# Four chained image layers on one core: the sparse last taps of two 3x3 convolutions as 64x64 products, beside two halves of a 1x1 mixing

## The chip, the core and the metric

The kernel runs on one core of a Trainium2 chip. A core has five engines, each with its own queue of instructions: TensorE (PE, matrix products; its weight loads are listed apart as PEld), VectorE (DVE), ScalarE (ACT), GpSimd (POOL) and SyncE (SP, which issues most DMA transfers). The engines wait for one another through semaphores. Operands lie in SBUF, 128 partitions wide; products accumulate in PSUM, also 128 partitions wide, of which the kernel uses eight banks of 512 fp32 columns (its pools add up to them).

The metric is the device time of one execution in microseconds (us). A trace records when each instruction and each DMA packet started and how long it took.

## The reference

Sixteen images of 64 channels and 128x128 pixels pass four layers. Each adds a function of its group-normalized input (32 groups of two channels) to its input:

```python
x = x + einsum('oc,bchw->bohw', conv_w, gram(gn(x)) applied to gn(x))   # layer 0: 1x1 mixing
x = x + abs(sobel_x(gn(x))) + abs(sobel_y(gn(x)))                       # layer 1: 3x3, per channel
x = x + conv3x3(shift(gn(x)), W) + b                                    # layer 2: quarter of channels
                                                                        # shifted left, quarter right
x = x + clip(leaky(batchnorm(conv1x1(conv3x3(gn(x), w_bin), w1x1))), 0, 255)   # layer 3
```

All is fp32. The batch normalization of layer 3 runs over all images, so its last part can only begin when every image has passed the products.

## The kernel before, in words

**Staging.** An image is cut into eight pieces (`NS`), and one step of the main loop (lines 1051 to 1099) works on one piece of each stage: `Front` (layers 0 and 1) of one image, `Layer2` of an image that is ten steps older, `Layer3` of one that is twenty steps older, and `Gram` (the Gram matrix of an image to come). A step has four quarters, `q` = 0 to 3. In each quarter the stages run in the order Layer3, Layer2, Front; then "last of" parts of Layer2 (quarters 0 and 3), then Gram, then `tick()`, which moves the chains of small statistics on by a link. Every engine executes in the order of the program (`InOrder`). When all images are through, a last loop normalizes, clips, adds and stores, bound to DMA.

**The products of layers 2 and 3.** Rows are worked in pairs, and a 3x3 kernel over pairs is written with sums and differences of planes: `difference` (DVE, line 698) puts into `d2` or `d3` the difference of two neighbouring planes, slot 0 and slot 1, and products of differences and of whole planes add up to the output `two` (two PSUM banks, slot 0 and slot 1). `one` is a third bank, for the shared plane (`shared`, three products on each half of the output channels). `own` (line 745) issues the products of one slot. Of the two output halves (64 partitions each) one has a whole 128x64 weight and takes three products, the taps kx = 1, 0, 2. The other half has only one plane with weights, so of its 128 weight rows 64 are zero. There, two taps are packed into one product (`pk`, which reads a copy of the difference, `qd`, the "twin", shifted by one pixel in one half), and the third, the **last tap**, remains a 128x64 product of which half the rows are zero. In all five products per slot.

**How products run.** A product of 64 output columns takes a half of the array; `issue` (line 722) holds products of both halves in queues and emits them in turns, so that two run side by side. `issue_rest` empties the queues before Front's products in quarters 1 and 3. An fp32 product appears in the trace as two passes.

**When.** Layer 3: `shared` and `own` of slot 0 in quarter 0, `own` of slot 1 in quarter 1; `y`, the sum read from `two` by DVE, in quarter 2, then the differences of the next piece in quarters 2 and 3. Layer 2: `shared` and `own` of slot 1 in quarter 2, `own` of slot 0 in quarter 3; the difference of slot 1 for the next piece ("last of 3", line 911) at the end of quarter 3; then, in quarter 0, the first two Sobel operations of the front, an addition at the row edges, `x`, the sum read from `two` (line 840), and the difference of slot 0. The twin of a layer 2 difference is made by two POOL-issued DMAs (line 802), that of layer 3 by two ACT copies. `d2`, `d3` and their twins have one buffer each.

**The mixing.** `abd` is a block-diagonal 128x128 weight (two copies of the 64x64 mixing, for the upper and lower half of the image). For the first three images (`EARLY`) `mix` issues whole 128x64 products, two in quarter 1 and two in quarter 3. For images 3 to 15 (`four`), `load` places a chunk so that rows 0 to 63 of the array get one four-row group of both image halves and rows 64 to 127 the other, and `mix_four` (line 571) issues four 64x64 products in quarter 1, one on each quadrant of the array: group 0 writes the bank `po`, group 1 the bank `g`. ACT normalizes them into `xh` (`prepare`): group 0 in quarter 2 of the same step, group 1 in quarter 0 of the next one.

Of the kernel before, what the change touches and what calls it, by code (L numbers as in the profile page):

```python
# [16 lines left out]
P = 128  # L17
# [3 lines left out]
R = 8  # L21
NS = HH // R
EARLY = 3
CP = 4
# [85 lines left out]
def tile_kernel(ctx: ExitStack, tc: tile.TileContext, x, cw_h, w2_t, b2, wbin_t, w1_t, b1, gamma, beta, consts, out):  # L110
# [56 lines left out]
    def cols(o):  # L167
        return slice(o * C, (o + 1) * C)
# [372 lines left out]
    class Front:  # L541
# [14 lines left out]
        def load(self, i):  # L556
            b = self.b
            t = xin.tile([P, R, W], F32, tag="x", name=f"x_{b}_{i}")
            if self.four:

                t = t.rearrange("p (h r) w -> p h r w", h=2)
                v = x[b].rearrange("c (h r) w -> c h (r w)", h=2)
                for g in range(2):
                    j = (i * R + g * CP) * W
                    sp.dma_start(t[cols(g)].rearrange("p h r w -> p h (r w)"), v[:, :, j:j + CP * W])
            else:
                for h in range(2):
                    sp.dma_start(flat(t[h * C:(h + 1) * C]), halves(x[b].rearrange("c h w -> (c h w)"), h, i * R, R))
            self.xs[i] = t

        def mix_four(self, i):

            for g, (pool, tag) in enumerate(((ps_po, "po"), (ps_g, "g"))):
                self.po[i, g] = pool.tile([P, CP, W], F32, tag=tag, name=f"po_{self.b}_{i}_{g}")
            t = self.xs.pop(i)
            order = 1 - last[0], last[0]
            for g in range(2):
                for h in order:
                    pe.matmul(self.po[i, g][cols(h)], self.abd[cols(g), cols(g)], t[cols(g), h], start=True, stop=True)

        def mix(self, i, g):
            if self.b == 0 and (i, g) in ((0, 1), (1, 0)):
# [15 lines left out]
        def at(self, i, q):  # L598
            b = self.b
            if q == 0:  # L600
                if i == -3:

                    self.xe = xin.tile([P, W], F32, tag="xe", name=f"xe_{b}", bufs=1)
                    sp.dma_start(self.xe[lo], x[b][:, HH, :])
                    sp.dma_start(self.xe[hi], x[b][:, HH - 1, :])
                    sp.dma_start(x2_d[b][0:W].rearrange("(p w) -> p w", p=1), w0[0:1, 0:W])
                if i + 3 < NS and i + 3 not in self.xs:
                    self.load(i + 3)
                if -1 <= i < NS - 1:
                    self.prepare(i + 1, 1)  # L610
                if 1 <= i:
                    self.store(i - 1)
                    act.activation(
                        junk.rearrange("p (j w) -> p j w", w=W), self.x2.pop(i - 1), AF.Square,
                        accum_out=self.st[:, 1, i - 1:i],
                    )
                if i == NS:
                    chains.append(coefficients(self.st, lambda co: coefs2.update({b: co}), b2_sb))
            if q == 1 and -2 <= i < NS - 2:
                if i == -2:  # L620
                    self.abd, self.co = lead.pop(b)
                if i == -2 and not self.four:
                    self.pe = ps_g.tile([P, CP, W], F32, tag="g", name=f"pe_{b}")[:, 0, :]
                    small_product(self.pe, self.abd, self.xe)
                if self.four:
                    self.mix_four(i + 2)
                else:
                    self.mix(i + 2, 0)
            if q == 3 and i == -2 and self.four:
                self.pe = ps_po.tile([P, CP, W], F32, tag="po", name=f"pe_{b}")[:, 0, :]  # L630
                small_product(self.pe, self.abd, self.xe)
            if (i, q) == ((-1, 0) if self.four else (-2, 2)):
                nc.gpsimd.memset(self.chunk(0)[lo, 0, :], 0.0)
                self.normalized(self.chunk(0)[hi, 0, 1:1 + W], self.pe[hi], hi)
                self.pel = small.tile([P, W], F32, tag="pel", name=f"pel_{b}", bufs=1)
                self.normalized(self.pel[lo], self.pe[lo], lo)
            if q == 2:
                if i == NS - 2:
                    nc.gpsimd.memset(self.chunk(NS - 1)[hi, R + 1, :], 0.0)
                    act.copy(self.chunk(NS - 1)[lo, R + 1, 1:1 + W], self.pel[lo])  # L640
            if 0 <= i < NS:
                self.sobel(i, q)
            if q == 2 and -2 <= i < NS - 2:
                self.prepare(i + 2, 0)
            if q == 3 and -2 <= i < NS - 2 and not self.four:
                self.mix(i + 2, 1)
                self.xs.pop(i + 2)

        def sobel(self, i, q):
# [69 lines left out]
        pe.matmul(dst, wt, src, start=start, stop=stop)  # L719
        last[0] = o  # L720

    def issue(halves):


        for o in range(2):
            for n, (dst, wt, src) in enumerate(halves[o]):
                held[o].append((dst, wt, src, n == 0, n + 1 == len(halves[o])))
        while held[0] and held[1]:
            o = 1 - last[0]
            emit(o)  # L730
            emit(1 - o)
# [10 lines left out]
    def shared(p, wt, t, m=CP):  # L742
        products(p[:, 0:m], [wt], [by_parity(t)[1][:, 0:m]])

    def own(p, n, table, wt, name, m=CP, both=None):
        d, q, pk = diffs[name][:, n, 0:m], twins[name][:, n, 0:m], packed[f"pk{name[1]}"][:, n]
        o, _ = single(table, n)
        some = [None, None]
        some[1 - o] = taps(1 - o, p[:, 0:m], [wt[:, n] if both is None else both], [d], 1)
        some[o] = [  # L750
            (p[cols(o), 0:m], pk, q[:, :, 1:1 + W]),
            (p[cols(o), 0:m, 0:W - 1], wt[:, n, 2, cols(o)], d[:, :, 2:1 + W]),
        ]
        issue(some)


    tiles3 = {}

    class Layer2:
# [65 lines left out]
        def at(self, i, q):  # L825
# [51 lines left out]
            if q == 2:  # L877
                if 0 <= i < NS:
                    t = self.v[i]
                    one = ps_one.tile([P, CP, W], F32, tag="one", name=f"one2_{b}_{i}")  # L880
                    two = ps_two.tile([P, 2, CP, W], F32, tag="two", name=f"two2_{b}_{i}")
                    self.p[i] = two, one
                    shared(one, self.wi[:, 0], t, m)
                    if closing:
                        small_product(one[:, m, :], w0, t[:, R, :])

                    both = self.wi[:, 1]
                    own(two[:, 1], 1, TO_SLOTS, w2, "d2", m, both)
                    if closing:

                        p = two[:, 1, m:CP]
                        issue([taps(0, p, [both], [t[:, R:R + 1, :]]), taps(1, p, [both], [t[:, R - 1:R, :]])])

                    self.c = ring.tile([P, CP * W], F32, tag="c2", name=f"c2_{b}_{i}", bufs=1)
                    act.activation(self.c, flat(one), AF.Identity, bias=self.co[:, 5:6])
                if 1 <= i < NS:
                    self.square(i - 1)
                if 1 <= i:
                    self.store(i - 1)
            if q == 3:  # L900
                if 0 <= i < NS:
                    t = self.v.pop(i)
                    two, one = self.p[i]
                    both = self.wi[:, 1]
                    own(two[:, 0], 0, TO_SLOTS, w2, "d2", m, both)
                    if closing:
                        p, srcs = two[:, 0, m:CP], [t[:, R - 2:R - 1, :], t[:, R - 1:R, :]]
                        issue([taps(0, p, [w2[:, 0], both], srcs), taps(1, p, [both, w2[:, 1]], srcs)])
            if q == "last of 0" and i == NS:
                self.square(i - 1)  # L910
            if q == "last of 3" and -1 <= i < NS - 1:
# [4 lines left out]
    class Layer3:  # L916
# [34 lines left out]
        def at(self, i, q):  # L951
# [10 lines left out]
            if q == 1:  # L962
                if 0 <= i < NS:
                    two, one = self.p[i]
                    own(two[:, 1], 1, TO_PAIRS, w3, "d3")
                    self.v.pop(i)
                    self.c = ring.tile([P, CP * W], F32, tag="c3", name=f"c3_{b}_{i}", bufs=1)
                    act.activation(self.c, flat(one), AF.Identity, bias=b1_sb)
                if i + 1 < NS:
                    self.prepare(i + 1)  # L970
                if 1 <= i:
                    y = self.y.pop(i - 1)
                    for s in range(2):
                        for z in range(2):
                            v = pairs(y_d[b], s)[:, (i - 1) * R:i * R, :].rearrange("c (n z) w -> c z n w", z=2)
                            sp.dma_start(v[:, z], y[s * C:(s + 1) * C, z])
# [74 lines left out]
    for step in range(starts[2][1] - 2, steps):  # L1051
        now[0] = step
        for q in range(4):
# [5 lines left out]
            for stage, at in starts:  # L1059
                if stage is Front and q in (1, 3):  # L1060
                    issue_rest()
                for b in range(B):
                    run(stage, b, step - at - NS * b, q)
            if q in (0, 3):
                for b in range(B):
                    run(Layer2, b, step - starts[1][1] - NS * b, f"last of {q}")
# [116 lines left out]
```

## Time and profile before

| | |
|---|---|
| runs of the kernel | 2716.34, 2716.12, 2712.99 us; median 2716.12 |
| the profiled execution | 2713.5 us |
| its span, first to last instruction | 2711.7 us |
| PE busy | 2146.4 us (79% of the span), 14804 passes |
| DVE busy | 2116.7 us (78%) |
| ACT busy | 2069.4 us (76%) |
| POOL busy | 1042.6 us (38%) |
| mean granted PE clock | 0.899 |
| HBM traffic | read 346.23 MB, written 268.44 MB |
| passes of the mixing in 64x64 products | 832, 615 ns each |

A line of a timeline gives the start in us from the span's first instruction, the duration, the engine, the line, the operation, the tile written and the tiles read, their shapes, and how many instructions are merged (x8); in square brackets stands the engine's idle time before it and what released it ("issue": nothing that the profile shows). Nearly all instructions have the line L73, that of the wrapper that keeps the order, so they are told apart by tiles: `d<-v` is a difference, `qd<-d` its twin, `two<-d,w`, `two<-d,wi` and `two<-qd,pk` are products of the slots (in layer 2 with `wi`, which has the normalization of the image folded in), `one<-v,w` and `one<-v,wi` begin layer 3 and layer 2 on PE, `po<-x,abd` is the mixing, `bank<-xw` a Gram product, `u` and `e` are the Sobel's tiles. Passes are pipelined: a pass of 512 columns lasts 0.59 us, and the next one of the same half starts 0.43 us after it.

The chain that ended last is no help here: followed back from the end it lies in the DMA-bound last part. The stage before it, from 330 to 2000 us, has to be read step by step.

### The profile page before, as it was taken

How to read it: one execution, taken by the hardware profiler on the slowest of the kernel's cores; microseconds unless marked ns; L12 is line 12 of the kernel's file. 1: busy time of each engine (PE TensorE's matmuls, PEld its weight loads, DVE VectorE, ACT ScalarE, POOL GpSimd, SP SyncE). 2: the span in 40 equal slices, each digit the busy share in tenths (PEclk: the TensorE clock that was granted, in tenths of full speed). 3: DMA queues.
4: the chain of work that ended last, by engine and by line, in shares of the span. 5: the costliest groups of instructions: out<-in, count | busy, mean ns of one | idle time of the engine just before them, and what ended most of it. 6: DMA issues, size and time to landing. Idle time of an engine off the chain costs nothing. (4 is left out here: it accounts for less than half of the span.)

```text
span 2711.7 us, 45518 instructions
## 1 busy us (share of the span) xinstructions
PE 2146.4 (79%) x14804; PEld 905.4 (33%) x14804; DVE 2116.7 (78%) x3111; ACT 2069.4 (76%) x3001; POOL 1042.6 (38%) x1558
## 2 busy tenths in 40 slices
PE   6578899999999999999999999999999992000000
PEld 4234433434343434343434343333335641000000
DVE  4998899898989898989898999999994335333332
ACT  4766889898989898989899989999996666333332
POOL 2266545444445454444445454655554300000000
PEclk8689999999999999999999999999999996555555
DMA  8799889998999889898989888888887879999999
GB/s 208 204 236 241 223 197 245 225 237 222 236 225 241 227 230 230 227 231 232 229 228 237 214 216 204 212 216 218 220 204 187 219 197 327 420 420 420 420 420 374
DMA packets 693596, 685.92 MB, mean 253 GB/s; under 512 B 60096, under 2 KB 580448, under 8 KB 693360
## 3 DMA queue, kind: packets, MB, share of 16 engines
q1 hardware_dynamic: 668208, 613.83, 79.0%
q0 software_dynamic: 25152, 69.18, 10.0%
q8 instruction: 119, 1.95, 0.3%
q14 instruction: 117, 0.96, 0.1%
HBM read 346.23 MB, written 268.44 MB: 227 GB/s over the span
## 5 line engine op out<-in xcount | busy, mean ns | idle before, releaser
L73 PE MATMUL two<-d,w 128*64 128x508 f32 (+2 forms) x2560 | 835.7, 586 | 0.0
L73 PE MATMUL two<-d,wi 128*64 128x508 f32 (+3 forms) x1536 | 571.7, 576 | 0.0
L73 PE MATMUL two<-qd,pk 128*64 128x512 f32 (+1 forms) x1024 | 517.4, 586 | 25.7 <-DMA qd<-d 25.3
L73 POOL DMA_DIRECT2D qd<-d x512 | 272.3, 534 | 686.5 <-DVE d L73 277.9
L73 POOL TENSOR_SCALAR edges<-v,co 64x8 f32<-64x8 f32 x512 | 328.7, 642 | 274.7 <-ACT v L73 195.1
L73 DVE TENSOR_TENSOR d<-v 128x512 f32<-128x512 f32 (+1 forms) x512 | 346.7, 680 | 86.0 <-issue 50.4
L73 PEld LDWEIGHTS two<-d,w 128*64 128x64 f32 x2560 | 272.4, 136 | 322.8 <-issue 282.7
L73 PE MATMUL one<-v,w 128*64 128x508 f32 (+2 forms) x1600 | 364.4, 579 | 1.1 <-ACT v L73 1.1
L73 PE MATMUL one<-v,wi 128*64 128x508 f32 (+3 forms) x1536 | 355.8, 595 | 0.4 <-DVE wi L73 0.3
L73 ACT COPY qd<-d 64x512 f32<-64x512 f32 x512 | 315.6, 616 | 23.3 <-DVE d L73 13.8
L73 DVE SCALAR_TENSOR_TENSOR e<-e 128x1032 f32<-128x1032 f32 (+1 forms) x256 | 313.3, 1224 | 0.0
L73 ACT ACTIVATE xh<-po,co 128x128 f32<-128x128 f32 (+1 forms) x480 | 275.5, 624 | 28.9 <-PE po L73 25.0
L73 PEld LDWEIGHTS two<-d,wi 128*64 128x64 f32 x1536 | 178.6, 135 | 201.3 <-issue 183.2
L73 POOL TENSOR_SCALAR v<-v,kc 128x9 f32<-128x9 f32 x256 | 229.9, 912 | 12.0
L73 DVE SCALAR_TENSOR_TENSOR y<-two,c 128x1024 f32<-128x1024 f32 x128 | 156.0, 1219 | 98.0 <-ACT v L73 45.5
L73 PE MATMUL po<-x,abd 64*64 64x512 f32 (+1 forms) x1024 | 176.6, 639 | 43.9 <-ACT xh L73 38.2
L73 ACT ACTIVATE v<-x,co 128x1024 f32<-128x1024 f32 (+3 forms) x256 | 203.9, 847 | 0.0
L73 ACT ACTIVATE u<-u 128x1024 f32<-128x1024 f32 x128 | 135.6, 1060 | 81.6 <-DVE u L73 80.1
L73 ACT ACTIVATE c<-one,co 128x512 f32<-128x512 f32 x128 | 87.0, 679 | 140.2 <-PE one L73 140.1
L73 PEld LDWEIGHTS two<-qd,pk 128*64 128x64 f32 x1024 | 135.2, 136 | 164.6 <-issue 104.8
L73 PEld LDWEIGHTS one<-v,w 128*64 128x64 f32 x1600 | 130.5, 136 | 175.9 <-issue 147.3
L73 DVE SCALAR_TENSOR_TENSOR u<-xh 128x1170 f32<-128x1170 f32 x128 | 175.5, 1371 | 5.6 <-ACT xh L73 4.5
(160 smaller groups left out, 3432.1 us busy)
## 6 DMA issues: line engine op xcount, KB each, us to landing
x<-in_x SPq DMA_DIRECT2D x256, 256.0 KB, 4.7
x_d<-u SPq DMA_DIRECT2D x512, 128.0 KB, 4.1
y_d<-y SPq DMA_DIRECT2D x512, 128.0 KB, 3.5
x_d<-x SPq DMA_DIRECT2D x496, 128.0 KB, 3.1
xr<-in_x SPq DMA_DIRECT2D x120, 512.0 KB, 6.0
qd<-d POOLq DMA_DIRECT2D x256, 130.0 KB, 3.2
qd<-d POOLq DMA_DIRECT2D x256, 129.8 KB, 3.8
v<-x_d SPq DMA_DIRECT2D x448, 72.1 KB, 2.8
```

The lines of the kernel that those rows point to most:

```text
L73: return self.tc.keep_in_program_order(call(*args, **kwargs))
```

## The change

The last taps leave `own`. `last_taps` collects them in a list, `sparse`, as soon as a layer's last slot is issued. `mix_four` no longer issues anything: for one four-row group it collects the two 64x64 products on the diagonal of the array (image half h to output half h, both into one bank) in the list `beside`, group 0 in quarter 1, group 1 in quarter 3. `issue_sparse`, after the stages of a quarter, issues both lists: the two last taps as 64x64 products with their 64 weight rows alone, which lie off the diagonal, then the two mixing products. So layer 3's last taps run with group 0 at the end of the second quarter, layer 2's with group 1 at the end of the fourth. Where nothing is mixed that way (the first three images, and after the front is through) the last taps are issued as a pair of 128x64 products, as before but at that later place. `load` places a chunk of every image as it did for the first three, in two transfers with runs of 4 KB instead of 2 KB. `issue`, `own` and the closing rows of layer 2 pass on whether an accumulation is still open.

```diff
-            if self.four:
-                t = t.rearrange("p (h r) w -> p h r w", h=2)
-                v = x[b].rearrange("c (h r) w -> c h (r w)", h=2)
-                for g in range(2):
-                    j = (i * R + g * CP) * W
-                    sp.dma_start(t[cols(g)].rearrange("p h r w -> p h (r w)"), v[:, :, j:j + CP * W])
-            else:
-                for h in range(2):
-                    sp.dma_start(flat(t[h * C:(h + 1) * C]), halves(x[b].rearrange("c h w -> (c h w)"), h, i * R, R))
+            for h in range(2):
+                sp.dma_start(flat(t[h * C:(h + 1) * C]), halves(x[b].rearrange("c h w -> (c h w)"), h, i * R, R))
...
-        def mix_four(self, i):
-            for g, (pool, tag) in enumerate(((ps_po, "po"), (ps_g, "g"))):
-                self.po[i, g] = pool.tile([P, CP, W], F32, tag=tag, name=f"po_{self.b}_{i}_{g}")
-            t = self.xs.pop(i)
-            order = 1 - last[0], last[0]
-            for g in range(2):
-                for h in order:
-                    pe.matmul(self.po[i, g][cols(h)], self.abd[cols(g), cols(g)], t[cols(g), h], start=True, stop=True)
+        def mix_four(self, i, g):
+            pool, tag = ((ps_po, "po"), (ps_g, "g"))[g]
+            po = pool.tile([P, CP, W], F32, tag=tag, name=f"po_{self.b}_{i}_{g}")
+            t = self.xs[i][:, g * CP:(g + 1) * CP, :]
+            for h in range(2):
+                beside.append((po[cols(h)], self.abd[cols(h), cols(h)], t[cols(h)], True, True))
+            self.po[i, g] = po
...
-                    self.mix_four(i + 2)
+                    self.mix_four(i + 2, 0)
...
-            if q == 3 and -2 <= i < NS - 2 and not self.four:
-                self.mix(i + 2, 1)
+            if q == 3 and -2 <= i < NS - 2:
+                if self.four:
+                    self.mix_four(i + 2, 1)
+                else:
+                    self.mix(i + 2, 1)
                 self.xs.pop(i + 2)
...
+    sparse, beside = [], []
+    def issue_sparse():
+        if beside:
+            for (dst, wt, src, o, i), other in zip(sparse, beside):
+                pe.matmul(dst, wt[cols(i)], src[cols(i)], start=False, stop=True)
+            for dst, wt, src, start, stop in beside:
+                pe.matmul(dst, wt, src, start=start, stop=stop)
+            last[0] = 1
+        else:
+            for dst, wt, src, o, i in sorted(sparse, key=lambda made: made[3] == last[0]):
+                pe.matmul(dst, wt, src, start=False, stop=True)
+                last[0] = o
+        sparse.clear()
+        beside.clear()
...
-        some[o] = [
-            (p[cols(o), 0:m], pk, q[:, :, 1:1 + W]),
-            (p[cols(o), 0:m, 0:W - 1], wt[:, n, 2, cols(o)], d[:, :, 2:1 + W]),
-        ]
-        issue(some)
+        some[o] = [(p[cols(o), 0:m], pk, q[:, :, 1:1 + W])]
+        issue(some, (False, False), [more or h == o for h in range(2)])
+    def last_taps(two, table, wt, name, m=CP):
+        for n in range(2):
+            o, i = single(table, n)
+            sparse.append((two[cols(o), n, 0:m, 0:W - 1], wt[:, n, 2, cols(o)], diffs[name][:, n, 0:m, 2:1 + W], o, i))
...
+                    last_taps(two, TO_SLOTS, w2, "d2", m)
...
                     own(two[:, 1], 1, TO_PAIRS, w3, "d3")
+                    last_taps(two, TO_PAIRS, w3, "d3")
...
                 for b in range(B):
                     run(stage, b, step - at - NS * b, q)
+            issue_sparse()
             if q in (0, 3):
```

## Prediction

> **What bounds the kernel now.** I read the page first. Over most of the span TensorE (PE), VectorE (DVE), ScalarE (ACT) and the DMA engines are all eight or nine tenths busy, so a share of busy time names no limit. Then I cut the trace into steps. A step is one round of the main loop: eight row pairs of the 3x3 layer ("layer 3" here, the fourth of the reference), eight of the shifted one ("layer 2"), one chunk of the front. It begins here where DVE starts layer 2's late difference, `difference("d2", 1)`. This is the windows view of the eight steps that handle one image (columns: length, busy us with instructions of PE, PE's weight loads, DVE, ACT, POOL, then PE clock, DMA share, GB/s):
>
> ```profile
> 969.10:983.70 14.60, 14.60 (x72) 4.88 (x70) 14.38 (x20) 14.50 (x23) 7.26 (x11) 1.00 0.88 244
> 983.70:998.60 14.90, 14.90 (x82) 4.91 (x80) 14.80 (x23) 14.81 (x23) 5.69 (x11) 1.00 0.83 201
> 998.60:1014.10 15.50, 15.50 (x152) 6.83 (x150) 15.24 (x27) 13.41 (x21) 7.51 (x12) 1.00 0.89 225
> 1014.10:1032.20 18.10, 18.10 (x170) 8.10 (x168) 16.32 (x27) 14.44 (x24) 5.66 (x10) 1.00 0.76 186
> 1032.20:1050.30 18.10, 18.10 (x178) 7.96 (x176) 15.74 (x28) 13.67 (x22) 8.18 (x13) 1.00 0.94 239
> 1050.30:1065.70 15.40, 15.40 (x99) 6.41 (x97) 14.63 (x23) 15.30 (x23) 10.80 (x16) 1.00 0.95 245
> 1065.70:1085.10 19.40, 19.40 (x118) 9.23 (x115) 15.89 (x26) 18.33 (x31) 8.59 (x12) 1.00 0.97 246
> 1085.10:1099.90 14.80, 13.10 (x66) 4.02 (x62) 14.73 (x24) 14.55 (x22) 8.16 (x11) 1.00 0.94 242
> sum 130.80, PE 129.10 PEld 52.34 DVE 121.72 ACT 119.02 POOL 61.84; mean PE 16.14 PEld 6.54 DVE 15.22 ACT 14.88 POOL 7.73
> ```
>
> PE is idle for 1.7 us of 130.8, DVE for 9.1, and DVE's idle time lies in three of the eight steps. So PE carries the image, and behind it DVE stands almost level: in five steps DVE is busy to within 0.8 us of the length. Where images need no more Gram products (1640 to 2000 us) the same cut gives 119.0 us, PE 118.94, DVE 116.94. A gain on PE therefore reaches the end only in part.
>
> How PE holds DVE up is seen in the timelines of DVE and then PE:
>
> ```profile
> 1030.61 0.08 DVE L73 DVE_READ_ACCUMULATOR u<-e,co,u 128x1 f32 x1
> 1032.21 0.69 DVE L73 TENSOR_TENSOR d<-v 128x512 f32<-128x512 f32 x1 [1.52 <-issue]
> ```
> ```profile
> 1029.39 0.59 PE L73 MATMUL two<-d,wi 128*64 128x512 f32 x1
> ...
> 1029.82 0.59 PE L73 MATMUL two<-d,wi 128*64 128x512 f32 x1
> ```
>
> A product is two passes; passes start 0.43 us apart and two products run side by side on the two column halves, so a pair of products is a slot of 0.85 us. Layer 2's late difference is read by three products of one half and two of the other, that is for three slots from 1029.38: the last pass starts at 1031.52 and ends 0.59 later, at 1032.1. At 1032.21 DVE overwrites the tile. That is the wait: DVE may run 1.6 us ahead of the end of layer 2's products (1033.8), not more.
>
> **The change, part by part.**
>
> *Products.* Per step and layer two last taps leave the slots (10 products in 5 slots become 8 in 4), so 16 slots become 14. The four 64x64 mixing products of the front, which ran as one group of four, become two groups, each with two taps. The price of a group is in this PE timeline:
>
> ```profile
> 1794.43 1.44 PE L73 MATMUL two<-d,w 128*64 128x508 f32 x5
> 1795.80 1.09 PE L73 MATMUL po<-x,abd 64*64 64x512 f32 x8
> 1796.82 1.93 PE L73 MATMUL one<-v,wi 128*64 128x512 f32 x8
> ```
>
> The last pass before the group starts at 1795.28 (1794.43 + 1.44 - 0.59); the group starts 0.52 later instead of 0.42, its successor 1.02 after it instead of 0.85, and the successor's passes need 1.34 us for three intervals instead of 1.27. So changing the shape of the array costs 0.10 + 0.17 + 0.06, about 0.3 us, and a group 1.15 us. Saved per step: 2 x 0.85 - 1.15 = **0.55 us of PE**, in the 104 steps that mix images 3 to 15 (at most 57 us). Elsewhere the taps stay pairs and nothing is saved.
>
> No trace of before shows a group with these positions. Before, each PSUM bank was written by one row half; now a mixing bank is written by both, in different partitions. Lower bound of the extra cost: nothing, since the old groups also wrote two partition halves of a bank at once (passes 7 ns apart). Upper bound: the two mixing products run one after the other, two more passes, 0.85 us per group. I take nothing, the nearer row.
>
> [...]
>
> *Release of the differences.* The last taps read `d2` at the end of the fourth quarter, so DVE's late difference now waits for layer 2's whole group: DVE may be 0 us ahead of it, not 1.6. The order of instructions on DVE shows the wait that stood before the edge addition, three instructions later, gone; the earlier one covers it. Queued behind the waiting difference on DVE are the next chunk's two Sobel operations (2.5 us), then `x`. PE doesn't need them at once: the twin of the difference is read 10 us later, and its DMA lands 3 to 4 us after issue. What is lost is the play between the two engines: a lag of PE can no longer be carried over 1.6 us from a step where DVE is longer. For layer 3 nothing moves: `y`, which waits for all its products, already stands ahead of the differences.
>
> *Moved mixing.* The second half of the mixing leaves the second quarter for the end of the fourth, just ahead of ACT's reading. ACT reads it at 1055.09 where layer 2 ended at 1051.9; 3 us of cover, price nothing. The chunk's tile is released later, and SP's load of the next waits for that, but SP reaches it at 1056.0, after the group. Behind it on SP are four stores. The load in pieces of 4 KB instead of 2 is worth under 0.2 us of DMA per step (129 ns per 2 KB packet, 233 per 4 KB). Nothing.
>
> *The sum over an image.* Between the starts of layer 3's first product PE needs 14.87, 15.06, 18.06, 17.94, 17.84, 15.6, 15.0 and 15.06 (the wait taken off); less 0.55 each. Now start DVE's late difference at 0 and layer 2's group at -0.3. PE ends at 14.0, 28.5, 46.0, 63.4, 80.7, 95.8. DVE, at the later of its own work (column DVE) and PE's end, comes to 14.4, 29.2, 46.0, 63.4, 80.7, 95.8. In the seventh step DVE waits for ACT:
>
> ```profile
> 1047.67 0.69 ACT L73 ACTIVATE c<-one,co 128x512 f32<-128x512 f32 x1 [4.33 <-PE one L73]
> ```
> ```profile
> 1074.20 0.17 DVE L73 TENSOR_REDUCE s<-st 128x2 f32<-128x16 f32 x1 [3.44 <-ACT junk L73]
> ```
>
> ACT works without a pause from 1047.67 to that square, 26.5 us, and was let go by PE. With the change it starts 4.4 us ahead of PE's 80.7 and ends at 102.8; DVE asks at 95.8 + 5.1 = 100.9 and waits 1.9 instead of 3.4. So 95.8 + 15.9 + 1.9 + 14.7 = 128.3 against 130.8: **2.4 us per image**, not 4.4. The same reckoning for the kernel before, with the play of 1.6 us and without the 0.55, gives back the starts read in the trace within 0.8 us.
>
> Images with Gram (78 steps, 9.75 images): 23 us. The 24 steps without: DVE needs 116.9, with about 0.7 of the wait for ACT 117.6 against 119.0, 4 us in all. The 12 early steps of layer 2 alone (187 to 331 us), where the first three images are mixed in whole pairs: nothing saved, and layer 2's last pair now follows the mixing, so the difference is released up to 1.62 + 0.85 us later. DVE is busy 129.0 of 143.4 us there, so between 0 and some 18 us is lost; I take 5. The end (DMA at 420 GB/s) just moves. 23 + 4 - 5 = 22: 2713.5 (profiled; span 2711.7) becomes 2691. That execution is 2.6 under the median of the runs, 2716.1; between the two, **2693**.
>
> **Rivals.**
>
> *Swallowed by DVE.* If ACT's 3.4 us stay and DVE binds in one more step, an image gains under 1 us, the early steps take it back: 2708 to 2719. For it: DVE's column. Against: PE's single idle time per image.
>
> *Late release: slower.* Place: DVE's late difference. If a new group costs 1.43 us, 0.28 more than the old one (half of the 2 x 0.85 + 1.15 = 2.85 that stood there), PE saves nothing and the lost play of 1.6 + 0.25 us is paid about once per image, 13 x 1.85 = 24, plus the early steps' 18: 2755; with half of that, 2735. The lost play, 42 us, is 0.4 us for each of the 104 steps, so it decides from about (2.85 - 0.4) / 2 = 1.2 us per group on. Against: groups all take 1.02 us in this trace.
>
> *One bank, two row halves.* The mixing products run in turn: per step 2 x 0.85 - 0.55 = 1.15 us more on PE, 104 times: 2830.
>
> **How the numbers follow.** Forecast (2666 to 2708) 0.62; swallowed 0.13; late release 0.16; serial bank 0.09. Faster 0.62, same 0.13, slower 0.25 by the bound of 0.2%, which is about what a measurement of this kernel can tell from no change. The low end is 4.4 us per image kept (43 + 6); the high end takes in the swallowed case and the mild half of the late release: 2666 to 2728.
>
> **What would show it.** Right: two groups of eight passes per step, each 1.02 us to its successor; steps of 17.5 where 18.1 stood; DVE's wait before the late difference still 1.4 to 1.7 us in Gram steps; the wait of `s` for ACT about 2 us. Wrong: passes of a group more than 0.1 us apart (bank), waits at the late difference in the 14.4 us steps or above 1 us more in the early ones (release), PE idle for more than 4 us per image with DVE full (swallowed).

## The result and the profile after

The changed kernel takes **2728.6 us** (median of 4 runs, 2728.2 to 2730.7); the kernel before, beside it on the same chip, 2714.6 us (4 runs, 2712.9 to 2716.3). The ratio is 1.0053, 95% interval 1.0036 to 1.0071: slower, where 2693 us had been forecast. The profiled execution took 2729.0 us, its span is 2727.2 us, 15.5 more than the span before.

The page of after, the row of engines; then the group of the differences in the page of before and in that of after (columns: count, busy us, mean ns, idle time just ahead and what ended most of it):

```profile
PE 2124.2 (78%) x14804; PEld 822.4 (30%) x14804; DVE 2116.4 (78%) x3111; ACT 2076.1 (76%) x3001; POOL 1095.9 (40%) x1558
```
```profile
L73 DVE TENSOR_TENSOR d<-v 128x512 f32<-128x512 f32 (+1 forms) x512 | 346.7, 680 | 86.0 <-issue 50.4
```
```profile
L73 DVE TENSOR_TENSOR d<-v 128x512 f32<-128x512 f32 (+1 forms) x512 | 347.3, 681 | 144.7 <-issue 87.6
```

PE is busy 22 us less (the prediction reckoned with 57 at most); DVE does the same work, but stands 59 us longer in front of its differences.

Where the 15.5 us arise is read by laying the two traces side by side at the same instruction. At the eleventh `x` of layer 2, the end of the early steps, after is 20.8 us behind, as the DVE timelines of before and then after show:

```profile
330.68 1.22 DVE L73 SCALAR_TENSOR_TENSOR x<-two,c 128x1024 f32<-128x1024 f32 x1
```
```profile
351.53 1.23 DVE L73 SCALAR_TENSOR_TENSOR x<-two,c 128x1024 f32<-128x1024 f32 x1
```

At the end of nine whole images with Gram products it is 18.0 behind, after the three images without 17.3, at the end 15.5. So the early steps lose more than the whole difference, and all later stages give back only 5.

The windows view of after, for the same image and with the same cuts as in the prediction (each row begins where DVE starts the late difference):

```profile
990.50:1004.90 14.40, 14.40 (x74) 4.31 (x76) 14.33 (x19) 12.44 (x19) 8.49 (x11) 1.00 0.92 261
1004.90:1019.70 14.80, 14.80 (x82) 4.49 (x80) 14.73 (x23) 14.71 (x23) 5.76 (x11) 1.00 0.83 211
1019.70:1036.70 17.00, 17.00 (x168) 7.24 (x166) 15.30 (x28) 15.50 (x23) 7.52 (x12) 1.00 0.86 216
1036.70:1054.00 17.30, 17.30 (x170) 7.25 (x170) 16.36 (x28) 14.43 (x24) 7.47 (x10) 1.00 0.79 199
1054.00:1071.50 17.50, 17.50 (x182) 7.56 (x180) 15.69 (x28) 13.85 (x22) 9.75 (x13) 1.00 0.91 220
1071.50:1087.10 15.60, 15.60 (x116) 7.22 (x114) 14.63 (x23) 15.50 (x24) 11.79 (x16) 1.00 1.02 257
1087.10:1104.50 17.40, 17.40 (x92) 5.89 (x92) 15.93 (x24) 16.36 (x27) 8.55 (x12) 1.00 1.01 264
1104.50:1120.00 15.50, 12.01 (x63) 3.58 (x60) 14.85 (x24) 15.20 (x23) 8.24 (x11) 1.00 0.85 222
sum 129.50, PE 126.01 PEld 47.55 DVE 121.82 ACT 117.99 POOL 67.57; mean PE 15.75 PEld 5.94 DVE 15.23 ACT 14.75 POOL 8.45
```

The two steps with most PE work became 0.8 and 0.6 us shorter, the seventh 2.0; but the third is 1.5 us longer and the eighth 0.7, with 3.5 us of idle PE in it (1.7 before).

For means over nine images a step is counted from one `y` (layer 3's evacuation on DVE) to the next, 0 to 7 in an image; all texts below count so. (Row n of the windows view ends with the late difference of step n - 1.) "Early" is from the first `x` to the eleventh. Mean lengths in us (each worked out from the trace of one execution):

| kernel | early | step 0 | 1 | 2 | 3 | 4 | 5 | 6 | 7 | image | image without Gram |
|---|---|---|---|---|---|---|---|---|---|---|---|
| before | 153.9 | 14.64 | 15.57 | 16.05 | 17.56 | 17.91 | 19.62 | 15.16 | 14.36 | 130.9 | 120.75 |
| after | 174.8 | 14.71 | 15.56 | 16.83 | 16.80 | 17.36 | 18.59 | 15.16 | 15.54 | 130.6 | 120.50 |

Steps 3, 4 and 5 gain 2.3 us, steps 2 and 7 lose 2.0.

**The early steps.** The timeline of DVE in before, one early step, where the late difference waits 1.3 us for POOL:

```profile
232.05 0.69 DVE L73 TENSOR_TENSOR d<-v 128x512 f32<-128x512 f32 x1 [1.30 <-POOL v L73]
```

The timelines of DVE, of PE and of ACT in after, one early step:

```profile
224.28 0.69 DVE L73 TENSOR_TENSOR d<-v 128x512 f32<-128x512 f32 x1 [3.40 <-issue]
224.89 1.37 DVE L73 SCALAR_TENSOR_TENSOR u<-xh 128x1170 f32<-128x1170 f32 x1
...
229.62 0.22 DVE L73 COPY gs<-pg 128x65 f32<-128x65 f32 x1
...
242.44 0.69 DVE L73 TENSOR_TENSOR d<-v 128x512 f32<-128x512 f32 x1 [5.02 <-issue]
```
```profile
229.94 0.70 PE L73 MATMUL pe<-xe,abd 128*64 128x128 f32 x4 [5.69 <-issue]
...
240.40 1.08 PE L73 MATMUL po<-x,abd 128*64 128x512 f32 x4 [0.19 <-ACT xh L73]
241.30 1.02 PE L73 MATMUL two<-d,w 128*64 128x508 f32 x4
```
```profile
233.30 1.06 ACT L73 ACTIVATE u<-u 128x1024 f32<-128x1024 f32 x1 [4.74 <-DVE u L73]
```

At 242.32 the last pair of layer 2 ends (`two<-d,w`, the four passes that the change put behind the mixing); 0.12 later DVE, idle for 5.02 us, writes the tile. Everything behind it on DVE starts late: the Sobel's `u`, the edges, `x`, the copy of the Gram product (229.62 to 229.84), which empties the bank that PE's `pe` writes at 229.94 after 5.69 us of idling, and ACT's |u| (4.74 us idle). These feed the products of the next step, whose end releases the next late difference. It is a closed loop of DVE, ACT and PE, 18.2 us from one late difference to the next, and no engine fills it, as the windows of two such steps in before and then in after show (PE busy 11 to 12 us, DVE 13; the number after POOL's is the clock that PE was granted):

```profile
217.62:232.05 14.43, 11.32 (x56) 4.65 (x54) 13.03 (x22) 11.18 (x16) 9.36 (x13) 0.88 0.99 244
232.05:246.11 14.06, 10.54 (x52) 3.54 (x50) 12.94 (x21) 12.06 (x17) 9.07 (x12) 1.00 1.03 278
```
```profile
224.40:242.50 18.10, 12.26 (x52) 4.51 (x52) 12.97 (x23) 11.92 (x18) 9.37 (x13) 0.81 0.91 232
242.50:260.30 17.80, 12.29 (x46) 4.04 (x48) 12.97 (x22) 12.65 (x18) 9.07 (x12) 0.81 0.78 206
```

PE also ran at half clock for 30.7 us of the early stretch in after, against 17.1 in before. That goes with its longer waits (up to 5.7 us from 190 to 330 us in after, up to 3.4 in before) and is not the cause: in run 7 below it ran so for 27.3 us, and the stretch took 153.4.

**The groups** cost what was forecast. The PE timeline of after:

```profile
822.58 0.54 PE L73 MATMUL two<-d,w 64*64 64x381 f32 x2
822.59 0.65 PE L73 MATMUL po<-x,abd 64*64 64x512 f32 x2
822.95 0.48 PE L73 MATMUL two<-d,w 64*64 64x381 f32 x2
823.07 0.59 PE L73 MATMUL po<-x,abd 64*64 64x512 f32 x2
823.60 2.78 PE L73 MATMUL one<-v,w 128*64 128x512 f32 x12
```

The first passes of two taps (here of 381 columns) and of two mixing products start within 0.02 us of one another, the second ones 0.37 and 0.48 us later, and the successor stands 1.02 us after the first pass; so it does at the median of 208 groups. Two row halves wrote different partitions of one PSUM bank side by side: the first passes of the two mixing products start 7 ns apart in all 208 groups.

### The profile page after: what moved, and what is told of

It reads as the page before. It is cut to its first block, busy times and chain, and to the rows that moved or that the text cites. A ratio compares the mean times of both kernels' runs of the same rounds, so it can differ in the third digit from the quotient of the medians.

```text
span 2727.2 us, 45364 instructions
## 1 busy us (share of the span) xinstructions
PE 2124.2 (78%) x14804; PEld 822.4 (30%) x14804; DVE 2116.4 (78%) x3111; ACT 2076.1 (76%) x3001; POOL 1095.9 (40%) x1558
## 5 line engine op out<-in xcount | busy, mean ns | idle before, releaser
L73 PE MATMUL two<-d,w 128*64 128x508 f32 (+3 forms) x2560 | 739.4, 597 | 0.0
L73 PE MATMUL two<-d,wi 128*64 128x508 f32 (+3 forms) x1536 | 485.0, 582 | 0.0
L73 DVE TENSOR_TENSOR d<-v 128x512 f32<-128x512 f32 (+1 forms) x512 | 347.3, 681 | 144.7 <-issue 87.6
L73 POOL TENSOR_SCALAR edges<-v,co 64x8 f32<-64x8 f32 x512 | 380.0, 742 | 187.0 <-ACT v L73 140.2
L73 PEld LDWEIGHTS two<-d,w 128*64 128x64 f32 (+1 forms) x2560 | 208.6, 135 | 390.0 <-issue 377.1
L73 PE MATMUL po<-x,abd 64*64 64x512 f32 (+1 forms) x1024 | 293.7, 652 | 40.0 <-ACT xh L73 37.1
L73 PEld LDWEIGHTS two<-d,wi 128*64 128x64 f32 x1536 | 153.4, 136 | 193.2 <-issue 187.6
L73 ACT ACTIVATE v<-v,co 128x1154 f32<-128x1154 f32 x128 | 172.3, 1346 | 6.9 <-DMA v<-x_d 5.9
L73 PEld LDWEIGHTS one<-v,w 128*64 128x64 f32 x1600 | 109.9, 137 | 218.0 <-issue 165.0
## 6 DMA issues: line engine op xcount, KB each, us to landing
x_d<-u SPq DMA_DIRECT2D x512, 128.0 KB, 4.1
y_d<-y SPq DMA_DIRECT2D x512, 128.0 KB, 3.7
x_d<-x SPq DMA_DIRECT2D x496, 128.0 KB, 3.3
```

Source lines behind the costliest of these rows:

```text
L73: return self.tc.keep_in_program_order(call(*args, **kwargs))
```

## The experiments

The theory: the whole loss is the late difference of layer 2, held until the last pass that reads its only buffer. Rivals: a group costs PE more than reckoned ("dear groups" in the expectations); the last pair waits for the mixing ahead of it, which waits for ACT; the twins land late.

**1. Last taps inside the layer in the steps without 64x64 mixing.**

```diff
+    def grouped():
+        return any(-2 <= now[0] - starts[2][1] - NS * b < NS - 2 for b in range(EARLY, B))
...
-        issue(some, (False, False), [more or h == o for h in range(2)])
+        if not grouped():
+            some[o].append((p[cols(o), 0:m, 0:W - 1], wt[:, n, 2, cols(o)], d[:, :, 2:1 + W]))
+            issue(some, (False, False), [more, more])
+        else:
+            issue(some, (False, False), [more or h == o for h in range(2)])
```
(`last_taps` returns at once in these steps, and a closing row ends its own accumulation.)

> The change, but in steps without 64x64 mixing the last taps stay where they were before, inside their slots. Late release (the loss sits in the 12 early steps of layer 2, 153.9 to 174.8 us from the first to the eleventh x): those steps return to 154 us, 19 us go, 2709 to 2711 us, ratio to the kernel before 0.998; the image steps stay as in the change (about 131 us per image, PE waiting 2.8 us for the twin's DMA in the eighth). Dear groups (the loss is the second change of shape per step): the early steps hold no group, so nothing goes, 2728 us.

Measured: 2705.2 us (2700.1 to 2707.5), ratio to before 0.9948 [0.9933, 0.9963]. Early 153.8 us, as before the change. So the late taps cost some 20 us where they save nothing, and the rest of the change is a gain. Images, whose program is the same as in the change, came to 129.5 us instead of the 130.6 there, mostly by steps 5 and 7 (18.07 and 15.07 us); that is some 9 us over nine images, and why was not taken apart.

**2. The kernel before, with the late taps in those steps alone** (`sparse` and `last_taps` as in the change, called only where `not grouped()`).

> The kernel before, with the last taps issued at the end of the quarter only in steps without 64x64 mixing; the four-fold mixing group is untouched. Late release: the early steps lengthen by the same 19 us, 2733 us, ratio 1.007. Dear groups or the new loads as the cause: no change, 2714 us.

Measured: 2741.8 us (2732.3 to 2744.8), ratio 1.0079 [1.0060, 1.0098]; early 176.9 us, images 131.5. The part by itself makes the whole loss: 23 us in the early steps, the rest in images whose program is that of before.

**3 and 4. The late difference moved behind `x`**, in the change and in run 1:

```diff
                 if 0 <= i < NS:
+                    difference("d2", 1, self.v[i], m)
+                    self.twin(1)
                     difference("d2", 0, self.v[i], m)
...
-            if q == "last of 3" and -1 <= i < NS - 1:
-                difference("d2", 1, self.v[i + 1], CP if i + 2 < NS else CP - 1)
-                self.twin(1)
```

> The change, with layer 2's late difference (slot 1) taken from the end of the fourth quarter to the first quarter, behind x, so that DVE has done the two Sobel operations (2.5 us) before it asks for the end of layer 2's products. Late release: the wait ahead of the late difference goes, of the early 19 us some 14 go, and the eighth step of an image, where DVE waited 2.3 us for the group that had waited for the twin of slot 0, loses 2 us: 2728.6 - 14 - 20 = 2695 us. The twin of slot 1 is made 3.6 us later; if that is late in the eighth step too, up to 1.5 us per image come back (2710). Dear groups: 2728 us, since PE does the same.

> Both edits: last taps inside their slots where nothing is mixed in 64x64 products, and the late difference behind x. Late release: 2709.6 from the first edit, less 20 for ten images: 2690 us (2690 to 2705). Dear groups: not under 2728 us.

Measured: 2764.0 us, ratio 1.0167 [1.0141, 1.0192], and 2754.9 us, ratio 1.0133 [1.0118, 1.0149]. Both expectations missed by far. The early stretch falls only to 169.4 us (159.7 in the second), and images grow to 134.3 (133.9). PE's waits between the ninth and the eighty-first `y` in before, then in run 3 (us in total, times, longest):

```profile
PE two L73 <- DMA qd<-d: 14.6, 9, 2.5
```
```profile
PE two L73 <- DMA qd<-d: 37.7, 22, 3.9
PE bank L73 <- DVE s L73: 7.1, 6, 1.5
```

Issued two Sobel operations and an `x` later, the difference and its twin reach PE late in the same step. Moved this far, the difference lacks the head start that it needs. (The edit also puts the early difference behind the late one; what each of the two costs was not parted.)

**5. The last pair ahead of the mixing** in steps without 64x64 mixing, to part the mixing's share from the layer's own:

```diff
                 if stage is Front and q in (1, 3):
                     issue_rest()
+                    if not grouped():
+                        issue_sparse()
```

> The change, but in steps without 64x64 mixing the two last taps of a layer are issued ahead of the mixing of the same quarter (which waits for ACT) and not behind it; they still stand behind all other taps of the layer. Theory A, the loop: the 20 us lost in the early steps come from the last pair standing behind the mixing, whose wait for ACT's xh stands behind abs(u), behind DVE's Sobel, behind the late difference that waits for the pair. Then the early stretch falls from 174.8 to 154-160 us and the time from 2728.6 to 2708-2714 (ratio to before 0.997-0.999). Rival B, the amount: the difference is released late by the number of passes ahead of it, and the mixing is only about a third of these; then the early stretch is about 168 us and the time about 2722. Images as in the change under both (130.5 us).

Measured: 2719.9 us (10 runs, 2714.1 to 2729.9), ratio 1.0007 [0.9995, 1.0019]. The profiled execution is the slowest of the ten; its early stretch is 169.3 us. Its timelines of PE and DVE:

```profile
222.18 1.03 PE L73 MATMUL two<-d,w 128*64 128x508 f32 x4
...
223.04 1.03 PE L73 MATMUL po<-x,abd 128*64 128x512 f32 x4
```
```profile
223.31 0.69 DVE L73 TENSOR_TENSOR d<-v 128x512 f32<-128x512 f32 x1 [2.62 <-issue]
```

The pair is now issued ahead of the mixing and ends at 223.21, and the difference follows at once, but DVE still waited 2.6 us for it. By the ratios 0.0046 of the 0.0105 between the change and run 1 come back, by the early stretches 5.5 of 21.0 us (rival B: 168 us and 2722; theory A: at most 160 us). So the mixing and its wait are the smaller share, a quarter to under a half; the rest is that the last reader stands behind all other products of its layer.

**6. Run 1 with two buffers in turn for the late difference**, so that DVE waits for no pass of the layer before; **7. the same buffers in the kernel before**, as a control.

```diff
+    other = wpool.tile([P, 1, CP, W + 2], F32, name="d2y")
+    pool.memset(other, 0.0)
+
+    def diff(name, n, turn=0):
+        return other[:, 0] if (name, n, turn) == ("d2", 1, 1) else diffs[name][:, n]
...
-                difference("d2", 1, self.v[i + 1], CP if i + 2 < NS else CP - 1)
-                self.twin(1)
+                difference("d2", 1, self.v[i + 1], CP if i + 2 < NS else CP - 1, (i + 1) % 2)
+                self.twin(1, (i + 1) % 2)
```
(The readers take `diff(name, n, i % 2)`; three small tiles of the Gram chain share tags to make room.)

> The change with last taps inside the layer in steps without 64x64 mixing (2705.2 us when measured), and in addition two buffers in turn for the late difference of layer 2 (slot 1), so that DVE's late difference waits for no pass of the layer before it. Theory A, release: steps 2 and 7 of an image, 0.85 and 0.7 us longer than before the change, are held by that release; both go back (16.05 and 14.4 us), images 128.0 us, total about 2690 us. Rival B, landing: step 7 is held by the landing of the early difference's twin (x waits for the group, the group for the twin's product), which a second buffer doesn't touch; then only step 2 gains, images 128.7 us, total about 2697. Rival C: the release costs nothing in images, 2705.

> The kernel before with two buffers in turn for the late difference of layer 2, a control for the run above. In before the late difference waits for the last pass of its slot 1.2-1.6 us less than in the change, and mostly for POOL's v in early steps; so the second buffer should bring next to nothing: 2713-2718 us, images 130.5-130.9 us. If the release was already on the path before the change, images fall to about 129.5 and the time to 2705.

Measured: 2693.6 us (2691.2 to 2697.0), ratio 0.9916 [0.9902, 0.9929]; the control 2713.6 us, ratio 0.9987 [0.9977, 0.9996]. Theory A holds, but for its size: steps 2 and 7 fall to 15.33 and 14.46 us, below and level with before. The mean wait of DVE for the late difference in steps 2, 3, 4, 5, 7 was 0.83, 1.70, 2.27, 0.08, 0.0 us in before and 1.61, 0.93, 1.73, 0.80, 1.10 in after; here, and in the control, it is at most 0.1. Of the 2.5 us that steps 2, 3 and 7 gain over run 1, step 5 takes back 1.9: there DVE waits longer for ACT, on average 2.6 us for a square against 1.3 in run 1, and 1.0 us for |u| against nothing. So images come to 129.0, not 128.0. In the control the 0.7 us that step 2 gains mostly return in steps 3 and 5.

**8. The change as it is, with the two buffers.**

> The change as it is, all steps with last taps at the end of the layer, and two buffers in turn for layer 2's late difference. Theory A: all that the change loses in the early steps (20.9 us) is DVE's late difference held until the last pass that reads its one buffer. Then the early stretch is back at 153-156 us and the time is 2693-2697 us, as with the taps kept inside in the early steps (2693.6). Rival B: the late taps delay something else as well there (x, which waits for the whole layer, or ACT's share); then the early stretch stays above 160 us and the time above 2702.

Measured: 2695.4 us (2693.2 to 2697.7), ratio 0.9917 [0.9901, 0.9933]; early 155.3 us. The groups of the differences (`d2y` is the second buffer), then two steps of the loop in the windows view:

```profile
L73 DVE TENSOR_TENSOR d<-v 128x512 f32<-128x512 f32 x448 | 304.7, 683 | 8.1 <-POOL v L73 8.1
L73 DVE TENSOR_TENSOR d2y<-v 128x512 f32<-128x512 f32 x64 | 41.7, 651 | 7.9 <-POOL v L73 7.9
```
```profile
216.31:231.63 15.32, 11.35 (x64) 4.29 (x59) 13.12 (x22) 11.89 (x17) 9.37 (x13) 1.00 0.95 237
231.63:245.69 14.06, 9.59 (x46) 3.20 (x48) 12.94 (x22) 11.80 (x17) 9.07 (x12) 0.98 0.94 243
```

Nothing of the change was undone: the taps are late, the mixing is split, the last pair stands behind the mixing. One more buffer of 2 KB per partition turned 0.5% slower into 0.8% faster; 144.7 us of idle time ahead of the differences became 16.0 (8.1 and 7.9), and it is spent on POOL's `v`, not on a release. The control, with the same buffers in the kernel before, gained 0.1%. That settles the cause of the loss: theory A. Not all the waiting went away; some moved behind work that DVE has meanwhile done. This is the edge addition behind the two Sobel operations, in after and in this run:

```profile
L73 DVE TENSOR_TENSOR two<-two,edges 128x16 f32<-128x16 f32 x128 | 22.5, 176 | 5.1 <-PE two L73 5.1
```
```profile
L73 DVE TENSOR_TENSOR two<-two,edges 128x16 f32<-128x16 f32 x128 | 22.1, 173 | 39.9 <-PE two L73 39.0 <-PE bank L73 0.8
```

**9. The last two Gram loads later and together; 10. later and apart**, both in run 1, for the wait of 2.8 us that PE has in step 7:

```diff
-                if m + 3 < NS:
+                if m < 3:
                     self.load(m + 3)
+            if 4 * i + q == 22:
+                self.load(6)
+                self.load(7)
```
(Run 10: load 6 at 22, load 7 at 26.)

> The change with last taps inside the layer in steps without 64x64 mixing (2705.2 us when measured), and the last two Gram loads of an image (512 KB each) issued two quarters later, behind the twin of the early difference in step 6 and not just ahead of it. Theory landing: the twin in step 6 lands in 4-5 us and not in 6.3-7.5, PE's wait of 2.8 us for it goes, step 7 falls from 15.07 to about 14.4 us, total about 2699. Rival release: step 7 stays at 15.1 whatever the landing, total 2705. Should the two loads together collide with the next twins, step 7 or 0 grows by up to 1 us: 2710.

> The change with last taps inside the layer in steps without 64x64 mixing (2705.2 us when measured), and the last two Gram loads of an image each issued in the third quarter of a step, one in step 6 and one in step 7, so that neither is just ahead of an early difference's twin and the two are not together. Theory landing: the twins land in 4-5 us in steps 6 and 7; step 7 is 14.36 us as in the run with both loads later, and step 0 stays at 14.6 (there 16.4); images 128.9 us, time 2698-2700. If the second load now falls on the next twin, step 0 is 15.2 or longer and the time 2705 or more.

The PE timeline of after in step 7, with POOL's issue of the twins and SP's of a Gram load (`xr`):

```profile
854.15 1.08 PE L73 MATMUL two<-qd,pk 128*64 128x512 f32 x1 [2.77 <-DMA qd<-d]
```
```profile
846.96 1.02 POOL L73 DMA_DIRECT2D qd<-d  x2 [3.98 <-issue]
```
```profile
846.60 0.53 SPq L73 DMA_DIRECT2D xr<-in_x  x1
847.24 1.17 SPq L73 DMA_DIRECT2D x<-in_x  x2
```

The twins (two transfers of 130 KB), issued 0.4 us after the 512 KB load, are awaited until 854.15. In run 9, with no `xr` there:

```profile
832.17 0.61 PE L73 MATMUL two<-qd,pk 128*64 128x512 f32 x1 [1.28 <-DMA qd<-d]
```
```profile
826.48 1.03 POOL L73 DMA_DIRECT2D qd<-d  x2 [3.99 <-issue]
```

Measured: run 9 2715.1 us, ratio 0.9988 [0.9980, 0.9997]; run 10 2701.9 us (2696.8 to 2706.7), ratio 0.9944 [0.9928, 0.9961]. In both, step 7 is 14.36 us as in before, and the early difference's twins in step 6 have landed 4.3 to 5.8 us after the issue of the first, not 6.3 to 7.5 as in run 1 (5.8 to 6.9 before the change, with the load in the same place; in all runs the ninth image is left out, whose twins land in 4.2 to 4.7 us). But run 9 put both loads ahead of the next twins (landing 7.1 to 8.4 us, and 9.7 where POOL issued the second one late), and step 0 rose from 14.62 to 16.43 us; in run 10 these twins took 6.0 to 8.1 us and step 0 15.05. So a late twin is needed for the loss in step 7, and so is the late release: in run 6 the twins still land after 5.5 to 7.2 us, and step 7 is 14.46. Either cure alone takes the step back. In step 0 the loads only moved the trouble, and run 10 can't be told from run 1 by time.

**11. Layer 3's taps alone beside the mixing**, layer 2's kept inside, the second half of the mixing alone:

```diff
-        if not grouped():
+        if not grouped() or name == "d2":
             some[o].append((p[cols(o), 0:m, 0:W - 1], wt[:, n, 2, cols(o)], d[:, :, 2:1 + W]))
```

> Half of the change: only layer 3's last taps stand beside the first half of the mixing (steps with 64x64 mixing); layer 2's stay inside the layer, and the second half of the mixing is issued alone, two products on the diagonal. By the prediction's prices (a group 1.15 us, a slot 0.85 us) a step then has two groups and one slot (3.15 us) where before it had one group and two slots (2.85 us): 0.3 us more in each of the three steps of an image that PE bounds, images 131.5-132 us, time 2722-2727. Layer 2's differences are released as before, so the early stretch is 154 us and steps 2 and 7 are as before the change (16.0 and 14.4 us). If a group of two products alone is cheaper than one of four (0.6 us), images are 130.0-130.9 and the time 2708-2716.

Measured: 2735.6 us (2733.8 to 2738.4), ratio 1.0065 [1.0047, 1.0083]; images 132.3 us, those without Gram 122.8. The PE timeline:

```profile
701.19 0.59 PE L73 MATMUL two<-d,w 64*64 64x508 f32 x2
701.20 0.60 PE L73 MATMUL po<-x,abd 64*64 64x512 f32 x2
701.73 2.80 PE L73 MATMUL one<-v,wi 128*64 128x512 f32 x12
...
709.84 1.08 PE L73 MATMUL po<-x,abd 64*64 64x512 f32 x4
710.85 2.78 PE L73 MATMUL one<-v,w 128*64 128x512 f32 x12
```

Two mixing products alone take 1.01 us to their successor, two mixing products and two taps 1.02 (medians of 104 groups each): the taps ride free, and a group is worth its price only with four products in it. The direction was right, the size not: step 3 grew by 0.51 and step 4 by 0.20 us, about the 0.3 expected each, but step 2 grew by 0.9 (its late difference waits 1.68 us, 0.85 more than in before, presumably since PE comes later), and images without Gram by 2.1. Why those grew so much was not taken apart.

## Why the prediction was wrong

*What bounds the kernel.* Right for images: the PE-bound steps 3 and 4 gain 0.76 and 0.55 us where 0.55 each were reckoned.

*Price of a group, one bank and two row halves.* Right: a group starts 0.52 us after the pass ahead of it and its successor 1.02 us later, as reckoned, with passes side by side in all groups. The upper bound of 0.85 us more per group, from which the 2830 us came, is shown by no run: the two row halves that write different partitions of one bank were not put in turn, the first passes of their products start 7 ns apart.

*Release of the differences.* **This step failed.** "Queued behind the waiting difference on DVE are the next chunk's two Sobel operations (2.5 us), then `x`. PE doesn't need them at once" counted only the twin as what PE needs, and closed the account with "What is lost is the play between the two engines". The queue behind a waiting instruction is needed in turn: the Sobel by ACT's |u|, ACT by the mixing, `x` and the Gram copy by PE, and these end in the products that release the next difference. The step asked who is waiting behind, but did not follow them once round. Put at the lost play and 5 us of early loss, the release cost 20.8 us in the early steps, and run 8, which takes the wait for it away, brings these back to within 1.4 us of before.

*The early steps.* "I take 5" out of "between 0 and some 18": measured 20.8 (run 2: 23). How the 18 came about isn't said (twelve delays of 2.47 us less the 14.4 us that DVE stood idle would be 15); either way DVE's idle time was taken for room that swallows delay. With a loop that nobody fills it is no room, and every step pays: DVE's waits for the late difference there were 1.7 to 5.0 us from the second on, against 0.5 to 2.6 before. The row that was nearest to the case stood in the prediction itself: a delay of 1.62 + 0.85 us per step, in a stretch where PE had no surplus of work to hide it.

*Images.* 2.4 us each were reckoned (the sum shown gives 2.5), 0.3 came. The reckoning let DVE start at the end of layer 2, but did not see that the steps that PE does not fill pay: step 2 (+0.78) by the wait for the release, and step 7 (+1.18), where a late twin holds PE and the release then follows the group behind it. With the release taken away (run 8) images gain 1.6 and the images without Gram 0.67 each (1.4 were reckoned); the rest lies in step 5, where DVE waits 2.9 us for ACT's square instead of the 1.9 reckoned.

*Moved mixing*, priced at nothing: run 8 keeps it, and is faster; no cost is seen, but none was measured by itself.

*The rivals.* "Late release" had the place and the sign, but not the condition: it was to decide from a price of 1.2 us per group on, and decided at the 1.15 that was forecast, since its price in the early steps does not depend on the group. Its milder time was 2735.

The forecast 2693 is about what comes out when the released tile has a second buffer (2693.6 in run 6, 2695.4 for the whole change in run 8). That the totals agree so closely is partly luck: the profiled execution of run 8 is 16.9 us shorter than that of before, and its images gain 1.6 and 0.67 us each where 2.4 and 1.4 were reckoned.

## What to carry to other kernels

When a product moves later, ask which single-buffered tile it is the last to read, who writes that tile, and what stands behind that write in its engine's order; then follow those until the chain returns to the moved product. Where the stages on that loop are less than full (here PE 12 of 18 us), every step can pay for the delay, and shares of busy time do not show it. Look first whether one more buffer fits: here it was worth 1.4% in the changed kernel and 0.1% in the kernel before.

## What the runs showed of the hardware that was not expected

PE's clock dropped around waits of about 2 to 3 us. The windows of after around the step 7 above (the number after POOL's is the granted clock):

```profile
848.00:853.60 5.60, 3.38 (x16) 1.03 (x12) 5.60 (x7) 5.38 (x8) 4.52 (x6) 1.00 0.87 228
853.60:860.50 6.90, 6.35 (x20) 1.41 (x22) 4.57 (x7) 6.81 (x13) 2.16 (x3) 0.51 0.92 257
860.50:866.00 5.50, 5.50 (x32) 1.61 (x28) 5.47 (x8) 4.45 (x6) 1.70 (x4) 1.00 1.00 300
```

After the wait of 2.77 us passes last 1.08 us instead of 0.59. Four of nine images have such a stretch in step 7 (3.41 or 6.83 us long, at waits of 2.24 to 3.05 us), and that step takes 16.0 to 16.8 us there, 14.3 to 15.0 in the others; before the change no image had one. PE's wait there grew from 1.7 us on average to 2.6. So most of the 1.18 us that step 7 lost lies in the images with half clock. But half clock alone need not lengthen the step: with the second buffer seven steps 7 have such a stretch (two in run 6, five in run 8), and six of them take 14.4 us, one 15.2.

The length of the wait does not decide by itself: in after a wait of 2.24 us (until 594.33) brought half clock and one of 2.80 (until 1117.80) did not, nor did one of 2.47 in before (until 835.51). In the traces of before and after all starts and ends of half clock between 160 and 1990 us lie whole multiples of 3.41 us apart. Cut into pieces of that length on this grid, the traces have 13 pieces at full clock with 2.07 us or more of idle PE, and half clock follows all of them; it follows none of the 1026 with 1.70 us or less, and one of the 9 between. The wait of 2.24 us has 2.07 us in one piece; that of 2.80 has 1.40 in each of two.

Two transfers of 130 KB that POOL issues right behind a 512 KB load have landed 6.5 to 7.3 us (after) and 6.3 to 7.5 us (run 1) after issue instead of 4.3 to 5.8 (runs 9 and 10); in run 9 the late landing (7.1 to 8.4 us) moved to the next step with the loads.
